# Taking means off weights by an added product, loading weights first, and asking for the last experts' rows sooner, in a fused audio transformer block on Trainium2

## The chip, the cores and the metric

The kernel runs on one core of one Trainium2 chip. The metric is the device time of one execution in microseconds (us). Runs are marked fast or slow by their granted TensorE clock and time; every run in this document is of the fast state. Within that state the time still moves by up to 6.6 us from run to run (a_fetch below), and why it does so is one of the things that this study is about.

## The reference, cut to what matters

64 clips of 80,000 samples are cut into 157 frames of 512 samples. Each frame is turned by an orthonormal DCT; then one layer with an attention-like read and one layer of experts follow, each behind a normalisation and with a residual.

```python
frames = x.reshape(64, 157, 512)              # after padding
h = einsum('bfh,kh->bfk', frames, DCT)        # 512 x 512
y = layernorm(h)
V = y @ Wv + bv; gate = sigmoid(y @ Wg + bg)  # 512 x 512 each
key, query = phases of tanh(y @ Wk), tanh(y @ Wq)   # 32 columns each
# ... causal read of V by key and query phases and by positions, mixed by gate
h = h + (read / norm) @ Wo + bo
z = layernorm(h)
scores = softmax(mean(z, frames) @ Wg2 + bg2); e = argmax(scores)   # one of 16 experts per clip
h = h + scores[e] * (z @ We[e] + be[e])       # 512 x 512 for each clip
```

## The kernel before

The 64 clips go in 16 groups of four. A group has five tiles of tokens (four of 128 and a ragged one, `TAIL`). All products are 32-bit, on TensorE; DVE (VectorE), ACT (ScalarE) and POOL (GpSimd) do the elementwise work. The frames' DCT is done with folds on DVE (`fold_once`, `fold_twice`: sums and differences of parts of a frame) and products with small tables (`embed`). In the code cuts, `bank` and `psum` give pieces of the memory that TensorE writes its products to, `value` is a tile's product with Wv, and `spread` and `scale` multiply a tile of frames by each token's factor of the normalisation (`rstd`). To apply Wv, Wk, Wq and Wg to the *frames* rather than to the DCT's output, the first group turns these weights by the same DCT once, and takes off their mean over the 512 inputs, so that the layer norm's mean need not be taken off the tokens. This happens in `through_dct`:

```python
    load_half(0, 0)                              # frames of group 0, first half
    dct_e = load("dct_e", [P, 2, P]); trig_o = ...; lift = ...
    raw_v = load_raw("wv", D)
    tables = ...                                 # the DCT tables
    load_half(0, 1)
    raw_kq = load_raw("wkq", 2 * F); ...; raw_g = load_raw("wg", D)

    def through_dct(raw, to, n, summed=False):
        if summed:
            ...                                  # two additions on GpSimd, for Wg
        ps = bank()[:, :n]
        ...
            for c in range(C):                   # C = 4 chunks of 128 inputs
                nc.tensor.matmul(ps, mean, raw[:, c], start=(c == 0), stop=(c == C - 1))
        sub(raw, raw, ps.unsqueeze(1).to_broadcast([P, C, n]))      # DVE, 2048 columns for Wv
        yield
        ...                                      # six DCT products, copied out by ACT
```

`first_values` interleaves this with the first group's embeddings, statistics and values; `first_gate` makes the first group's four gate parts beside the embeddings of group 1:

```python
    def first_gate():
        made = chain(weight_sums(wo, t_o), weight_sums(wv, t_v), weight_sums(wg, t_g))
        for n in range(NM):
            embed(1, n)
            embed_statistics(1, n)
            if n == 0:
                fold_twice(1, 1)
            if n < C:
                gate_part(0, n)
            embed_res(1, n)
            ...
```

At the end of a group, an expert is picked for each clip, and its weights (1 MB each) are fetched by indirect DMA, issued by GpSimd with row numbers that DVE works out. For the last group nothing is left to hide this behind, so its four weights come in eight halves:

```python
    def picks(c):
        if c == 1:
            route_spread(g)
            pick(g)
    ...
    expert(g - 1, ORDER[2], picks)               # third expert tile of the group before
    spare = ...
    fetch(g, [...], parts=2)                     # rows on DVE, eight gathers on GpSimd
    pick_gate(g)
    bias(g)                                      # ninth gather, the experts' biases
    for n in (3, 4):
        add_bias(g - 1, ORDER[n])
        expert(g - 1, ORDER[n])
    last = psum()
    banks = [*(bank() for _ in range(3)), last[:, 0, :], last[:, 1, :]]
    for c in range(C):                           # chunk outside, tile inside
        for n in range(NM):
            if c == 0:
                add_bias(g, n)
            expert_chunk(g, n, c, banks[n])
            if c == C - 1 and n != 3:
                for m in (n,) if n < 3 else (3, 4):
                    expert_out(g, m, banks[m])
```

Of the kernel before, what the change touches and what calls it, by code (L numbers as in the profile page):

```python
# [14 lines left out]
F32 = mybir.dt.float32  # L15
# [36 lines left out]
def audio_tower(ctx: ExitStack, tc: tile.TileContext, a, out):  # L52
# [79 lines left out]

    load_half(0, 0)
# [3 lines left out]

    def load_raw(name, n):
        t = p1.tile([P, C, n], F32, tag="we", name=name, bufs=GB)
        nc.sync.dma_start(out=t, in_=a[name])  # L140
        return t

    raw_v = load_raw("wv", D)
    tables = p1.tile([P, 6, P], F32, tag="we", name="tables", bufs=GB)
    nc.sync.dma_start(out=tables, in_=a["tables"])
    load_half(0, 1)
    raw_kq = load_raw("wkq", 2 * F)
# [38 lines left out]
    def through_dct(raw, to, n, summed=False):  # L186




        if summed:
            total = p1.tile([P, 2, n], F32, tag="x2T", name="total")
            nc.gpsimd.tensor_tensor(total, raw[:, :2], raw[:, 2:], ALU.add)
            nc.gpsimd.tensor_tensor(total[:, 0], total[:, 0], total[:, 1], ALU.add)
            yield
        ps = bank()[:, :n]
        if summed:
            nc.tensor.matmul(ps, mean, total[:, 0], start=True, stop=True)
        else:
            for c in range(C):  # L200
                nc.tensor.matmul(ps, mean, raw[:, c], start=(c == 0), stop=(c == C - 1))
        sub(raw, raw, ps.unsqueeze(1).to_broadcast([P, C, n]))
        yield
        for k, parts in enumerate((((0, 1), (1, 3)), ((2, 1), (3, 3)), ((4, 0),), ((5, 2),))):
            if k % 2 == 0:
                ps = psum()
            for i, (table, r) in enumerate(parts):
                nc.tensor.matmul(
                    ps[:, k % 2, :n], tables[:, table], raw[:, r], start=(i == 0), stop=(i == len(parts) - 1)
                )  # L210
            if k % 2:
                nc.scalar.copy(to[:, k - 1 : k + 1], ps[:, :, :n])  # L212
                yield
# [396 lines left out]
    def output_product(g, i):  # L610
# [11 lines left out]
        elif i == 6:  # L622
            add(first, ps, first)
        elif i == 7:
            add(second, ps, first)
            more(r22, second)
            more(r21, second)
            more(r12, first)
        elif i == 5:
            add(r22, ps, r22)  # L630
            for n in (2, 3):
                statistics2(g, n)
            add(r12, ps, r12)
        elif i == 3:
            add(r12, ps, r12)
        else:
            add(r21, ps, r21)
# [76 lines left out]
    def fetch(g, rooms=(), parts=1):  # L714
# [6 lines left out]
        for k in range(parts):  # L721
            rows = t("rows", [P, GB], I32)
            base = rowbase[:, parts + k - 1 : parts + k]
            nc.vector.tensor_scalar(rows, s["rev"], float(-P * parts), base, ALU.mult, ALU.add)
            for b in range(GB):
# [78 lines left out]
    def first_values():  # L804

        consts = constants()
        turn_v = through_dct(raw_v, wv, D)
        turn_kq = through_dct(raw_kq, wkq, 2 * F)
        turn_g = through_dct(raw_g, wg, D, summed=True)

        def embedded(n):
            embed_statistics(0, n)
            embed_res(0, n)

        warm(20)
        fold_once(0, 0, nc.vector)
        fold_twice(0, 0)
        embed(0, 0)
        embed(0, 1)
        embedded(0)  # L820
        next(turn_v)
        embedded(1)
        next(turn_v)
        next(turn_v)
        fold_once(0, 1, nc.vector)
        value(0, 0)
        fold_twice(0, 1)
        keep_value(0, 0)
        embed(0, 2)
        embedded(2)  # L830
        value(0, 1)
        spread(0, 0)
        scale(0, 0)
        embed(0, 3)
        keep_value(0, 1)
        embedded(3)
        embed(0, TAIL)
        embedded(TAIL)
        next(turn_g)
        next(turn_kq)  # L840
        value(0, 2)
        spread(0, 1)
        scale(0, 1)
        next(turn_kq)
        next(turn_kq)
        keep_value(0, 2)
        value(0, 3)
        spread(0, 2)
        scale(0, 2)
        next(consts)  # L850
        keep_value(0, 3)
        value(0, TAIL)
        spread(0, 3)
        scale(0, 3)
        keep_value(0, TAIL)
        spread(0, TAIL)
        scale(0, TAIL)
        fold_once(1, 0)
        next(turn_g)
        project(0)  # L860
        fold_phases(0)
        next(turn_g)
        next(turn_g)
        next(consts)
        fold_twice(1, 0)
        fold_once(1, 1)
        phasors(0)
        next(consts)
        next(consts)
        weigh()  # L870

    def first_gate():

        made = chain(weight_sums(wo, t_o), weight_sums(wv, t_v), weight_sums(wg, t_g))
        for n in range(NM):
            embed(1, n)
            embed_statistics(1, n)
            if n == 0:
                fold_twice(1, 1)
            if n < C:  # L880
                gate_part(0, n)
            embed_res(1, n)
            add_bo(0, n)
            if n < C:
                for _ in range(3):
                    next(made)
            if n > 0:
                spread(1, n - 1)
                scale(1, n - 1)
            if n == 1:  # L890
                scores(0)
        load_half(2, 0)
        load_half(2, 1)

    def project_and_values(g):
# [5 lines left out]
        made = token_sums(g)  # L901
        next(made)
# [18 lines left out]
        keep_product(g)  # L921
        route(g - 1)
        route_sum(g - 1)
        value_product(g, 5)
        keep_product(g)
        route_spread(g - 1)
# [60 lines left out]
    def attention(g):  # L987
# [11 lines left out]
        for i in (1, 2, 6, 7, 4, 5, 3):  # L999
            output_product(g, i)  # L1000
            if i == 1:
# [4 lines left out]
                if g == 0:  # L1006
# [174 lines left out]
```

## Time and profile before

| | |
|---|---|
| time, median of 3 | 1436.16 us (1435.90 to 1436.41) |
| span of the profiled run | 1433.1 us, mean granted clock 0.997 |
| opening: start to the first output product of group 0 | 99.53 us |
| middle: from there to the same product of the last group | 1263.98 us |
| tail: from there to the end | 69.64 us |

I cut the span at two landmarks, the first product of Wo with gated values in the first group and in the last. They stand in the trace of every kernel here (line 361 before, line 362 in the changed kernel), so the three parts can be compared between kernels: opening, middle, tail. The tail holds the last group's output, its routing, the experts of the two last groups and the last stores.

A line of a timeline reads: start, length, engine, line of the kernel, operation, result and operands, shape, number of instructions, and in brackets how long the engine had stood idle ahead of it and what ended that. A line of the table of stretches has the stretch, its length, the busy time and instructions of PE, PEld, DVE, ACT and POOL, the granted clock, the DMA share and GB/s.

### The profile page before, as it was taken

The page shows a single profiled execution, that of the slowest core. Times are in us where ns is not written, and L with a number is a line of the kernel's source. Part 1 is how long each engine was busy: PE and PEld are TensorE (multiplying, and loading weights), DVE is VectorE, ACT ScalarE, POOL GpSimd, SP SyncE. Part 2 cuts the span into 40 slices and gives each one's busy share as a digit, 9 for nine tenths or more (in the row PEclk, how much of TensorE's full clock was granted, in tenths as well). Part 3 has the DMA queues.
Part 4 walks back from the last instruction along what each step waited for, and adds up shares of the span by engine and source line. Part 5 has one row for each costly group of instructions (what it writes and reads, how often), then busy time and mean ns, then how long its engine had stood idle before and what let it go on. Part 6 is the DMA issues. An engine that isn't in the chain of part 4 may idle for free.

```text
span 1433.1 us, 26995 instructions
## 1 busy us (share of the span) xinstructions
PE 1409.2 (98%) x10662; PEld 929.6 (65%) x10662; DVE 995.8 (69%) x2088; ACT 401.0 (28%) x691; POOL 607.3 (42%) x849
## 2 busy tenths in 40 slices
PE   8989999999999999999999999999999999999997
PEld 5567586675757657586675757657585675757751
DVE  4677676777767677676777767677677777767562
ACT  1414233142421314232142422314232142422310
POOL 2355443545445255433535445255433535445222
PEclk9999999999999999999999999999999999999999
DMA  6012304132040322304132040322304132030305
GB/s 210 1 38 78 113 9 148 52 125 74 5 179 16 126 74 86 108 7 157 42 125 74 13 171 16 126 74 95 102 3 163 36 126 74 22 126 16 125 17 182
DMA packets 46941, 119.47 MB, mean 83 GB/s; under 512 B 9232, under 2 KB 26144, under 8 KB 38752
## 3 DMA queue, kind: packets, MB, share of 16 engines
q0 software_dynamic: 11072, 71.31, 13.1%
q1 hardware_dynamic: 35244, 45.80, 10.8%
q8 instruction: 85, 1.39, 0.4%
q10 hardware_dynamic: 500, 0.64, 0.2%
q14 instruction: 40, 0.33, 0.1%
HBM read 97.14 MB, written 20.58 MB: 82 GB/s over the span
## 4 chain that ended last, share of the span: by engine, by line
PE 90%; DVE 4%; POOL 3%; issue 1%; ACT 1%; DMA 1%; DVEq 0%; POOLq 0%
PE mm L361 27%; PE mm L772 16%; PE mm L566 16%; PE mm L600 9%; PE mm L232 8%; PE mm L670 3%; PE mm L513 2%; PE mm L247 2%; PE mm L249 2%; POOL rstd L224 1%; PE mm L680 1%; PE mm L585 1%; DVE st L219 1%; PE mm L287 1%; POOL rstd L223 1%
## 5 line engine op out<-in xcount | busy, mean ns | idle before, releaser
L223 POOL TENSOR_SCALAR rstd<-mv 128x1 f32<-128x1 f32 x160 | 54.4, 340 | 547.9 <-DVE mv L221 535.1
L772 PE MATMUL mm<-we,x2T 128*32 128x512 f32 x2400 | 273.2, 595 | 0.8 <-DVE res_t L783 0.8
L772 PEld LDWEIGHTS mm<-we,x2T 128*32 128x32 f32 x2400 | 70.4, 109 | 149.5 <-issue 142.9
L97 DVE TENSOR_TENSOR gT<-mm,gT 128x128 f32<-128x128 f32 (+1 forms) x135 | 87.0, 673 | 89.8 <-PE mm L566 88.4
L608 DVE TENSOR_TENSOR gT<-mm,gT 128x320 f32<-128x320 f32 x256 | 116.8, 487 | 20.9 <-PE mm L600 16.5
L600 PE MATMUL mm<-att,v 32*128 32x192 f32 (+2 forms) x2048 | 128.0, 371 | 1.3 <-ACT res_t L276 1.0
L600 PEld LDWEIGHTS mm<-att,v 32*128 32x128 f32 x2048 | 105.8, 185 | 12.1 <-PE mm L600 3.0
L726 POOL DMA_INDIRECT we<-in_we,rows x60 | 64.3, 1072 | 103.9 <-issue 98.1
L97 DVE TENSOR_TENSOR v<-mm,v 128x512 f32<-128x512 f32 x105 | 71.0, 688 | 53.4 <-PE mm L361 53.4
L576 ACT ACTIVATE gT<-gT,hbg 128x320 f32<-128x320 f32 x120 | 59.6, 554 | 169.4 <-DVE gT L97 169.4
L224 POOL TENSOR_TENSOR rstd<-rstd,power 128x1 f32<-128x1 f32 x160 | 99.0, 619 | 13.3
L97 DVE TENSOR_TENSOR res<-mm,res 128x512 f32<-128x512 f32 x96 | 64.3, 684 | 56.7 <-POOL res L615 41.8
L276 ACT ACTIVATE res<-mm,shift,rstd 128x512 f32<-128x512 f32 x64 | 49.7, 777 | 165.6 <-POOL rstd L262 124.1
L783 DVE SCALAR_TENSOR_TENSOR res<-mm,gate,res 128x512 f32<-128x512 f32 x64 | 48.1, 751 | 61.6 <-PE mm L287 36.6
L657 ACT ACTIVATE x<-res,shift,rstd 128x512 f32<-128x512 f32 x64 | 52.1, 815 | 137.9 <-DVE res L97 121.3
L361 PE MATMUL mm<-t_o,sum 128*128 128x256 f32 x384 | 88.4, 379 | 0.0
L361 PE MATMUL mm<-t_v,sum 128*128 128x256 f32 x360 | 86.7, 384 | 0.0
L281 POOL TENSOR_TENSOR res<-res,bo 128x512 f32<-128x512 f32 x64 | 86.5, 1380 | 0.2 <-issue 0.2
L361 PEld LDWEIGHTS mm<-t_o,sum 128*128 128x128 f32 x384 | 71.9, 190 | 11.3 <-DVE sum L96 0.4
L615 POOL TENSOR_TENSOR res<-res,u 128x512 f32<-128x512 f32 x48 | 59.6, 1269 | 44.9 <-DVE u L97 44.9
L232 PE MATMUL mm<-wv,xT 128*128 128x512 f32 x160 | 72.2, 594 | 1.3 <-ACT wv L212 0.8
L361 PEld LDWEIGHTS mm<-t_v,sum 128*128 128x128 f32 x360 | 64.8, 190 | 10.7 <-issue 3.7
(195 smaller groups left out, 2770.2 us busy)
## 6 DMA issues: line engine op xcount, KB each, us to landing
xT<-in_frames SPq DMA_DIRECT2D x32, 640.0 KB
out<-res SPq DMA_DIRECT2D x248, 64.0 KB
out<-res_t SPq DMA_DIRECT2D x62, 32.0 KB
out<-res_t SPq DMA_DIRECT2D x62, 26.0 KB
wv<-in_wv SPq DMA_DIRECT2D x1, 1024.0 KB
wg<-in_wg SPq DMA_DIRECT2D x1, 1024.0 KB
wo<-in_wo SPq DMA_DIRECT2D x1, 1024.0 KB
we<-in_we,rows POOLq DMA_INDIRECT x60
```

The costliest lines, as they stand in the source:

```text
L97: add = lambda *x: nc.vector.tensor_tensor(*x, ALU.add)
L223: nc.gpsimd.tensor_scalar(rstd, mv[:, 1:2], EPS, None, ALU.add)
L224: nc.gpsimd.tensor_tensor(rstd, rstd, power, ALU.pow)
L232: nc.tensor.matmul(ps, tile_of(x[:, c], n), w[:, c, :], start=(c == 0), stop=(c == C - 1))
L281: nc.gpsimd.tensor_tensor(r, r, bo, ALU.add)
L361: nc.tensor.matmul(ps[:, b, :], lhs[:, c, P * b : P * (b + 1)], w[:, c, :], start=(c == 0), stop=(c == 1))
L566: nc.tensor.matmul(ps[:, o, :HN], w[:, c, o * P : (o + 1) * P], rhs[:, c], start=(c == 0), stop=(c == 1))
L576: nc.scalar.activation(to, to, AF.Tanh, bias=hbg[:, c : c + 1], scale=0.5)
L600: nc.tensor.matmul(to, s["v", n][q, c * P : (c + 1) * P], by, start=(n == 0), stop=(n == TAIL))
L608: nc.vector.tensor_tensor(th, r[:, :, n], th, op)
L726: nc.gpsimd.indirect_dma_start(out=ws[b][:, n * k : n * (k + 1)], out_offset=None, in_=of, in_offset=bass.IndirectOffsetOnAxis(ap=rows[:, ...
L772: nc.tensor.matmul(ps[Q * i : Q * (i + 1), :], s["x2T"][:, c, i, Q * n : Q * (n + 1)], s["ws"][i][:, c, :], start=(c == 0), stop=(c == C - 1),
```

## The change

The intent is to have TensorE start on real work sooner and wait less in the opening, and to have the last group's expert weights arrive sooner. It has six parts:

1. Tables and Wv are loaded ahead of the frames; Wv in two halves, the odd chunks first.
2. Wv and Wkq go through the DCT as loaded. Their mean comes off at the end: DVE adds up the four chunks, and one more product per output part, with the tables' sums over minus 512, accumulates in the same bank. Wg keeps its subtraction.
3. The order of the first group's work and of its gate parts changes; the gate part comes ahead of the embedding in `first_gate`.
4. DVE's four sums of Wg for the fast products (`t_g`) move from the first gate into group 1.
5. The last group's gathers are requested inside `picks`, with the bias gather between the halves.
6. The last block takes two chunks for all tiles, then the other two tile by tile, the ragged tile first. In the last group one addition (`r12`) stands ahead of two statistics.

```diff
+    tables = p1.tile([P, 6 + C, P], F32, tag="we", name="tables", bufs=GB)
+    nc.sync.dma_start(out=tables[:, :6], in_=a["tables"])
+    raw_v = load_raw("wv", D, (slice(1, C, 2), slice(0, C, 2)))
     load_half(0, 0)
 ...
+    nc.sync.dma_start(out=tables[:, 6:], in_=a["table_sums"].partition_broadcast(P))
+    raw_kq = load_raw("wkq", 2 * F)
     load_half(0, 1)
 ...
+    def less_mean(total, k, to):
+        nc.tensor.matmul(to, tables[:, 6 + k], total, start=False, stop=True)
+
+    def centre(raw, total):
+        ps = bank()
+        nc.tensor.matmul(ps, mean, total, start=True, stop=True)
+        sub(raw, raw, ps.unsqueeze(1).to_broadcast([P, C, D]))
 ...  (first_values)
+        for k in range(2):
+            through_dct(raw_v, k, of[k], stop=False)
+        total = add_up(raw_v, D, "x2T")
+        for k in range(2, C):
+            through_dct(raw_v, k, of[k], stop=False)
+        total_kq = add_up(raw_kq, 2 * F, "sum2")
         fold_once(0, 0, nc.vector)
         fold_twice(0, 0)
+        for k in range(C):
+            less_mean(total, k, of[k])
 ...  (first_gate)
+        made = chain(weight_sums(wo, t_o), weight_sums(wv, t_v))
+        for n in range(C):
+            gate_part(0, n)
             if n == 0:
                 fold_twice(1, 1)
+            m = n + 2
+            if m < NM:
+                embed(1, m)
 ...  (the last group)
     def picks(c):
         if c == 1:
             route_spread(g)
             pick(g)
+            fetch(g, [*flat, all_v.rearrange("p i c o -> p (i c o)")], 2, biases)
 ...
-    fetch(g, [*flat, all_v.rearrange("p i c o -> p (i c o)")], parts=2)
-    pick_gate(g)
-    bias(g)
 ...
+    order = [TAIL, *range(TAIL)]
+    for c in range(2):
+        for n, ps in zip(order, banks):
+            expert_chunk(g, n, c, ps)
+    for n in order:
+        add_bias(g, n)
+    for n, ps in zip(order, banks):
+        for c in range(2, C):
+            expert_chunk(g, n, c, ps)
+        expert_out(g, n, ps)
```

## The prediction

> **What bounds the kernel now.** I read the page first. TensorE is busy nearly all the span and the chain that ended last lies on it.
>
> ```profile
> PE 1409.2 (98%) x10662; PEld 929.6 (65%) x10662; DVE 995.8 (69%) x2088; ACT 401.0 (28%) x691; POOL 607.3 (42%) x849
> ...
> PE 90%; DVE 4%; POOL 3%; issue 1%; ACT 1%; DMA 1%; DVEq 0%; POOLq 0%
> ```
>
> So an average tells nothing here: only TensorE's work, or the little time it waits, can change the time. The busy table by stretches of time says where it waits (columns: stretch in us; its length; busy us of the five engines; granted clock; DMA share; GB/s).
>
> ```profile
> 7.70:99.50 91.80, 80.27 (x503) 50.48 (x503) 59.41 (x125) 27.27 (x46) 38.11 (x60) 0.98 0.23 80
> 99.50:1402.20 1302.70, 1300.58 (x9961) 867.86 (x9959) 926.36 (x1949) 372.49 (x644) 563.55 (x776) 1.00 0.24 81
> 1402.20:1408.60 6.40, 3.74 (x14) 0.45 (x11) 0.00 (x0) 0.00 (x0) 4.69 (x5) 0.90 0.99 345
> ...
> 76.10:79.50 3.40, 3.40 (x7) 2.20 (x8) 3.28 (x7) 0.06 (x1) 1.19 (x3) 0.50 0.02 5
> ```
>
> The reader is to see that 1300.6 of the middle 1302.7 us are busy: fifteen of sixteen groups offer nothing. The waits lie in the first group (up to 99.5 us) and after 1402 us, and twice the clock falls to 0.50. The timeline of TensorE names the waits (start, length, instructions, idle before).
>
> ```profile
> 16.58 5.42 PE L208 MATMUL mm<-wv,tables 128*128 128x512 f32 x12 [2.38 <-DVE wv L96]
> 49.66 2.37 PE L513 MATMUL mm<-xT,wkq 128*64 128x320 f32 x16 [0.73 <-DVE xT L293]
> 76.06 6.26 PE L547 MATMUL mm<-xT,wg 128*128 128x320 f32 x16 [3.87 <-ACT res L276]
> 93.48 1.40 PE L600 MATMUL mm<-att,v 32*128 32x320 f32 x22 [0.99 <-ACT res_t L276]
> 99.53 1.99 PE L361 MATMUL mm<-wo,gT 128*128 128x256 f32 x8
> ...
> 1402.53 1.02 PE L772 MATMUL mm<-wv,x2T_last 128*32 128x512 f32 x2 [0.28 <-DMA wv<-in_we,rows]
> 1405.43 1.05 PE L772 MATMUL mm<-wg,x2T_last 128*32 128x512 f32 x2 [1.88 <-issue]
> 1406.97 1.60 PE L772 MATMUL mm<-spare,x2T_last 128*32 128x512 f32 x2 [0.50 <-issue]
> ```
>
> The first line is the pass that takes the means off Wv: DVE subtracts for 2.3 us while TensorE stands. The line at 99.53 marks the end of the first group's opening, 99.53 us. The last three are the last group's expert weights arriving one by one. The timeline of DVE and GpSimd shows why they come late:
>
> ```profile
> 1395.45 0.75 DVE L783 SCALAR_TENSOR_TENSOR res<-mm,gate,res 128x512 f32<-128x512 f32 x1 [1.43 <-PE mm L772]
> 1396.12 0.35 DVE L724 TENSOR_SCALAR rows<-rev,rowbase 128x4 int32<-128x4 f32 x2
> ...
> 1397.13 1.07 POOL L726 DMA_INDIRECT wv<-in_we,rows  x1 [11.45 <-DVE expf L743]
> 1398.51 1.05 POOL L726 DMA_INDIRECT wg<-in_we,rows  x1 [0.30 <-issue]
> ```
>
> The expert was picked at 1394.02, but the row numbers stand in DVE's queue behind an addition that waits for TensorE.
>
> **What the Trainium skill says.** "TensorE: Matmul & The Clock Gate", Part 1: the clock is judged in free-running windows of 3413 ns, an idle window halves it for the next. The trace agrees: both 0.50 stretches last 3.41 us, follow an idle stretch (3.87 us; 6.3 us with three short bursts), and stretch 16 passes at line 547 from 4.47 to 6.26 us. "GPSIMD Engine Reference", 3.1: a 2048-element fp32 addition takes DVE 2293 ns, GpSimd 4497. The trace has 2.29 us for the DVE subtraction of 2048, 2.34 us on GpSimd for 1024: agreed. "DMA: Bandwidth & Descriptors", Anatomy of one DMA: about 2.0 us plus bytes / 436e3. That gives 3.2 us for a half gather of 512 KB; here the first took 5.4 us (1397.13 to 1402.53) and the fourth 7.5. The measurement decides.
>
> **The change part by part.** I list the queues of the built program, with what each instruction waits for, and lay durations of this trace on them.
>
> *Mean of Wv and Wkq.* Before: 4+4 matmuls with the mean matrix ahead, then a DVE subtraction. After: 4+4 correction matmuls behind, accumulated in the same bank. A 128x512 matmul is two passes of 0.43 us, so 4 x 0.86 = 3.44 us go and 3.44 come: no work is saved, but the 2.4 us wait and 2.29 us of DVE go. What DVE adds is 1.3 + 0.7 us of sums, beside the six DCT matmuls (5.2 us).
>
> *Load order.* Tables (384 KB) and Wv's halves (512 KB each) now precede the frames. The before trace moves about 350 to 400 KB per us from 2.3 us on and reports landings some 0.6 to 1.3 us after the bytes. So tables and first half land near 5.3, the second half near 6.8, the frames near 8.6, the table sums near 10.6, Wkq near 11.0. Warm-up falls from 40 to 24 passes and ends near 5.5 (14 cold at 0.21, 10 at 0.11). TensorE then starts real work at about **5.6** instead of 7.72, and its ten Wv matmuls run to 14.2, under which the fold of the frames (3.7 us of DVE from 11.5, held by Wkq's sum) nearly hides.
>
> *TensorE work from there to line 361's first product*, the same in both: Wv 8.6, Wkq 2.3, five values 17.2, ten embeddings 8.9, spreads 1.1, Wg 6.0, projection 2.3, position scores and scores 2.0, four gate parts 17.2, read 7.5; sum 73.2. Before: 99.53 - 7.72 - 73.2 = 18.6 us of waits and slow clock.
>
> *Waits I expect after.* First tile's second trig matmul 0.3. Values 2 and 3 wait for the scaling of tile 0, for res of tile 2 and res of tile 3: 0.9 + 0.5 + 0.8. The Wg subtraction (kept, 2.29 us on DVE) now stands before the last spread and ahead of the value it must keep: 3.0. That gap fills a clock window, so 1.7 us of slow clock at 8 in 10: 1.4. Tile 2 of group 1 needs fold_twice of the second half, which stands on DVE behind both statistics and behind weigh, that is behind eight Sin activations (4.2 us after a 1.28 us table load): TensorE ends gate part 0 near 60, the fold comes near 62.5 to 64: 3.4, and slow clock at even odds: 0.8. Start of the read, behind the last scalings: 1.5. Wake-ups: 0.9. Sum 13.5. Line 361 then starts at 5.6 + 73.2 + 13.5 = 92.3: **7.2 us gained**. The wait of 3.87 us moves and shrinks rather than vanishes.
>
> *t_g sums* (4 x 0.68 = 2.7 us of DVE) move from the first gate into group 1's value products. There DVE has gaps of 0.5 and 1.6 us and TensorE does not wait on what is delayed by 1.4 us; I charge 0.2.
>
> *Last gather.* Rows come after the pick: 1394.06 instead of 1396.12, so all gathers start 2.06 us earlier. The bias gather goes between the halves (+1.24 us for the second), but the second half is used 8.6 us after the first. TensorE starts the last block at 1406.5 by the old clock, not 1408.57: 2.1. The slow clock there cost 1.1 (two pass pairs at 0.855 and one at 0.65 instead of 0.43); with a shorter gap at even odds: 0.5.
>
> *Last block in another order.* Work is the same 20 x 0.86 us. Before, two tiles' outputs (4 + 8 transfers) hung on the last matmul: its DVE addition is at 1427.02, a second one follows, then six issues on each queue until 1430.7. After, one tile with two issues per queue: 1427.02 + 0.75 + 0.9 + 2.1 to land + 0.8 to close, about 1431.5 against 1433.1: 1.6. Tail: **4.2 us gained**. The earlier r12 addition I count as nought: its gain is a bank's release, its cost 0.7 us on two statistics.
>
> Sum: 7.2 + 4.2 - 0.2 = 11.2; with half a us given for later small shifts, 1436.2 - 11.7 = 1424.5.
>
> **Rivals.** (1) DVE becomes the bound of the opening: it is busy 59.4 of 91.8 us, and the new order stacks Wkq's sum, two statistics and the constants ahead of what TensorE needs. For it: the two new waits of 3 us. If they double, 1430 to 1432. (2) All waits of the opening go, as the change intends: then line 361 starts near 82 and the time is about 1414. Against: the Wg subtraction is still there. (3) The tail is bound by the gather's transfers, not its start: the DMA share is 0.99 from 1402 to 1408. If bytes alone set it, an earlier start still moves them, since the engines carried only 83 to 240 GB/s before 1400; so I keep most. If not, 1427.
>
> **Range and chances.** The opening may gain 3 to 12 us, the tail 2 to 5.5; together 5.5 to 17.5, so 1418.5 to 1430.5 holds it 8 times in 10. Faster by 2% needs 28.7 us; all waits outside the middle are 18.6 in the opening, 7.4 before the last block and 6 at the end, so nearly all would have to go: 0.01. Slower by 2% would need damage in the steady groups, whose order is unchanged: 0.005.
>
> **What would show it.** Right: the first matmul on Wv's raw tiles near 5.6; line 362 (old 361) near 92; a TensorE wait of about 3 us on the Wg subtraction near 42 to 45 and of 3 us on the fold near 60 to 64, with 0.50 clock behind the first; the first of the last gathers 2 us earlier against the last group's picks; the last addition to the end shorter by 1.6. The middle groups stay at their 86 to 87 us each. Wrong: if table sums or the second half of Wv land late and TensorE waits before 14 us; if the waits near 44 or 62 are absent; if the middle groups change.

## The result, and the profile after

| | before | after |
|---|---|---|
| median of 4 runs | 1436.29 us (1435.90 to 1440.82) | 1424.24 us (1423.01 to 1425.31) |
| ratio of the fast runs | | 0.9909, 95% interval 0.9887 to 0.9930 |
| span of the profiled run, clock | 1433.1 us, 0.997 | 1421.9 us, 0.998 |
| opening / middle / tail | 99.53 / 1263.98 / 69.64 us | 93.64 / 1263.65 / 64.65 us |

A ratio is the mean time of one kernel's fast runs over the mean time of the other's in the same rounds, so it is not quite the ratio of the medians. The measured 1424.24 us is 0.3 us from the predicted 1424.5; the range and the class (within 2%) held.

First the page of the changed kernel: its busy times, and the engines' shares of the chain that ended last.

```profile
PE 1405.3 (99%) x10646; PEld 929.2 (65%) x10646; DVE 997.3 (70%) x2090; ACT 402.0 (28%) x690; POOL 607.1 (43%) x849
...
PE 91%; DVE 3%; POOL 3%; DMA 1%; issue 1%; ACT 0%; SPq 0%; DVEq 0%; POOLq 0%
```

TensorE's busy time fell by only 3.9 us (1409.2 to 1405.3), part of it warm-up (sixteen passes fewer) and part time at half clock. The rest of the 11.2 us is idle time gone. The busy table by stretches says where:

```profile
7.00:93.64 86.64, 79.25 (x505) 50.54 (x505) 61.06 (x127) 27.89 (x45) 37.70 (x60) 0.98 0.27 90
93.64:1357.29 1263.65, 1262.31 (x9683) 847.70 (x9681) 902.72 (x1895) 366.82 (x635) 550.15 (x754) 1.00 0.24 82
...
1395.60:1400.30 4.70, 3.08 (x13) 0.36 (x8) 0.75 (x1) 0.00 (x0) 3.11 (x4) 1.00 0.95 334
...
65.30:68.70 3.40, 3.40 (x8) 2.42 (x9) 0.83 (x3) 2.44 (x4) 0.00 (x0) 0.50 0.00 0
```

The middle is as full as before. Idle time in the opening fell from 11.5 (91.8 less 80.3) to 7.4 us. The stretch between the arrivals of the first and the fourth expert weight is 4.7 us long at full clock; before it was some 6 us with the clock at 0.90. There is one stretch of half clock in the opening, as before, but in another place. The timeline of TensorE names what waits are left in the opening:

```profile
7.00 5.50 PE L196 MATMUL mm<-wv,tables 128*128 128x512 f32 x12 [0.15 <-DMA wv<-in_wv]
...
45.62 0.30 PE L288 MATMUL mm<-ident,rstd 128*128 128x128 f32 x1 [2.36 <-DVE wg L96]
46.19 5.42 PE L196 MATMUL mm<-wg,tables 128*128 128x512 f32 x12 [0.28 <-DVE v L411]
63.85 0.84 PE L248 MATMUL mm<-dct_e,xT 128*128 128x128 f32 x4 [2.63 <-issue]
```

The 2.38 us wait for DVE's subtraction from Wv, ahead of line 208 before, is gone, and Wv's DCT now begins at 7.00 instead of 16.58 us. The two waits that the prediction named are there: for the subtraction from Wg (2.36 and 0.28), and near 61 us for the fold of group 1's second half (2.63; the profile shows no releaser for it, and the built program has the instruction wait for that fold on DVE and for a bank that ACT frees). In the tail, the row numbers and gathers of the last group:

```profile
1387.55 0.41 DVE L728 TENSOR_SCALAR rows<-rev,rowbase 128x4 int32<-128x4 f32 x2
...
1388.57 1.07 POOL L732 DMA_INDIRECT wv<-in_we,rows  x1 [8.73 <-DVE logit L744]
...
1393.68 0.95 POOL L762 DMA_INDIRECT be<-in_be,expi  x1 [0.30 <-issue]
```

The rows now follow right behind the pick (its last step ends at 1387.51); before they stood 2.1 us behind it in DVE's queue. Measured from the last group's first output product, the first gather is issued at 31.28 us instead of 33.62. TensorE still waits for the halves, but shortly:

```profile
1396.85 1.04 PE L778 MATMUL mm<-wg,x2T_last 128*32 128x512 f32 x2 [0.27 <-DMA wg<-in_we,rows]
1398.80 1.05 PE L778 MATMUL mm<-spare,x2T_last 128*32 128x512 f32 x2 [0.90 <-DMA spare<-in_we,rows]
1400.28 0.62 PE L778 MATMUL mm<-t_v,x2T_last 128*32 128x512 f32 x1 [0.44 <-DMA t_v<-in_we,rows]
```

So in these two profiles 5.9 us came out of the opening, 0.3 out of the middle and 5.0 out of the tail. A pair of profiles is one draw of the clock's windows, though, and the experiments show that this draw is worth several us.

### The profile page after: what moved, and what is told of

The parts are those of the page before. It is cut to its first block, busy times and chain, and to the rows that moved or that the text cites. A ratio compares the mean times of both kernels' runs of the same rounds, so it can differ in the third digit from the quotient of the medians.

```text
span 1421.9 us, 26962 instructions
## 1 busy us (share of the span) xinstructions
PE 1405.3 (99%) x10646; PEld 929.2 (65%) x10646; DVE 997.3 (70%) x2090; ACT 402.0 (28%) x690; POOL 607.1 (43%) x849
## 4 chain that ended last, share of the span: by engine, by line
PE 91%; DVE 3%; POOL 3%; DMA 1%; issue 1%; ACT 0%; SPq 0%; DVEq 0%; POOLq 0%
PE mm L362 26%; PE mm L567 16%; PE mm L778 16%; PE mm L601 9%; PE mm L233 8%; PE mm L674 3%; PE mm L514 2%; PE mm L248 2%; PE mm L250 2%; PE mm L684 1%; POOL rstd L225 1%; PE mm L586 1%; PE mm L548 1%; PE mm L288 1%; DVE st L220 1%
## 5 line engine op out<-in xcount | busy, mean ns | idle before, releaser
L119 POOL TENSOR_TENSOR xT<-xT 128x640 f32<-128x640 f32 x30 | 46.5, 1550 | 59.7 <-DVE even L97 40.7
```

## The experiments

Twelve kernels ran, in three calls on three chips, each with five rounds and a profile. The kernel before ran beside them; its mean was 1437.1, 1438.2 and 1437.5 us. This table has all of them, with the time as median, and the parts of the one profiled run. "Slow" lists the starts of the stretches of half clock in that profile up to the last matmul.

| kernel | median us | ratio to before, 95% | opening | tail | slow from, us |
|---|---|---|---|---|---|
| before (profile) | | | 99.53 | 69.64 | 76.1, 1407.3 |
| after (profile) | 1424.24 | 0.9909 (0.9887 to 0.9930) | 93.64 | 64.65 | 65.3 |
| a_open | 1428.56 | 0.9939 (0.9926 to 0.9952) | 94.92 | 69.21 | 45.9, 66.4, 1401.0 |
| a_tail | 1434.38 | 0.9977 (0.9962 to 0.9992) | 103.08 | 65.97 | 16.9, 40.8, 78.3, 95.4 |
| a_fetch | 1435.91 | 0.9993 (0.9975 to 1.0011) | 103.41 | 70.92 | 17.6, 41.5, 79.0, 96.1, 1413.6 |
| a_block | 1434.82 | 0.9988 (0.9971 to 1.0004) | 99.51 | 69.97 | 76.2, 1407.4 (two windows) |
| again | 1425.21 | 0.9904 (0.9888 to 0.9920) | 95.20 | 64.67 | 46.2, 66.7 |
| b_fold | 1423.99 | 0.9900 (0.9883 to 0.9917) | 93.64 | 64.47 | 47.0 |
| b_wg | 1422.27 | 0.9890 (0.9873 to 0.9908) | 92.59 | 64.32 | 63.7 |
| b_both | 1422.60 | 0.9889 (0.9871 to 0.9906) | 92.05 | 66.34 | 1398.4 |
| u_fetch | 1425.62 | 0.9921 (0.9907 to 0.9935) | 95.00 | 68.94 | 46.3, 66.8, 1401.4 (two windows) |
| u_mean | 1431.90 | 0.9960 (0.9946 to 0.9974) | 102.75 | 65.09 | 9.9, 16.7, 54.3, 74.7 |
| u_load | 1429.13 | 0.9942 (0.9929 to 0.9955) | 98.90 | 65.16 | 9.4, 50.3, 70.8 |
| c_fill | 1423.51 | 0.9906 (0.9890 to 0.9921) | 92.19 | 65.09 | none |

The middle took 1263.94 to 1263.98 us in the kernels with the old opening and 1263.53 to 1263.69 in those with the new one. The 0.38 us lie in the first group alone (86.25 against 85.87 us; every later full group takes 85.83 to 85.84 in both): group 1's ragged tile was spread there before, and is now spread in the opening. So no gain or loss hides in the steady groups, and the theory that the moved `t_g` sums give the opening's gain back falls.

### Which half of the change did it: a_open and a_tail

My theory was that the gains of the opening and of the tail are independent and add up. The rivals were luck of the clock windows, and, for the tail, the transfers' own time. a_open is the changed opening with the old tail, a_tail the old opening with the changed tail.

```diff
 a_open, against the changed kernel
-            fetch(g, [*flat, all_v.rearrange("p i c o -> p (i c o)")], 2, biases)    # and parts 5 and 6 undone
+    fetch(g, [*flat, all_v.rearrange("p i c o -> p (i c o)")], parts=2)
 a_tail, against the kernel before
+            if g + 1 == NG:
+                add(r12, ps, r12)
+            fetch(g, [*flat, all_v.rearrange("p i c o -> p (i c o)")], 2, biases)    # and the block's new order
```

> The opening of the changed kernel (load order, means by an added pass, gate order, sums in group 1) with the tail of the kernel before (late gather, old order of the last block, old place of the r12 addition). Theory, gains add up: the first output product stands at 93.6 us as in the changed kernel, the tail takes from there what it takes before, so the time falls by 5.9 us, to about 1430.3 (ratio 0.996). Rival A, the tail's gain was luck of the clock windows: then this kernel comes out well below 1430, near 1425 to 1428, when its windows fall well. Rival B, the opening's gain is given back by the t_g sums in group 1: then the stretch from the first output product to the last group's is longer than 1264 us and the time is above 1432.

> The opening of the kernel before with the whole tail of the changed one (early gather, biases between the halves, last block in the other order, r12 addition earlier in the last group). Theory: the gain is that of the two profiles' tails, about 5 us, to 1431.0; of it about 1.8 from the gather, 1.1 from a slow clock that does not come, 1.85 at the very end, 0.5 from the r12 addition. Rival, clock luck: the slow clock comes back at the last block in this kernel's profile and the gain is 1.1 us less, near 1432.2. Rival, bytes: the last piece of weights lands as late as before, and only the end's 1.85 us remain, near 1434.

Measured: a_open has the ratio 0.9939, some 8.8 us of 1437; a_tail 0.9977, some 3.3 us. Together that is 12.1 us, and the whole change took off 13.1 (0.9909) and, in its repetition, 13.8 (0.9904). Within their intervals of about 2 us the halves add up, and the opening is the larger half. The amounts are not those that I expected from the two profiles (5.9 and 5): the opening gives more, the tail less. For a_tail the median, 1434.38 us, is the number of the rival with the transfers (near 1434) and not that of the theory (1431.0).

The profile of a_tail shows one cause of the larger opening. Its opening is that of the kernel before, instruction for instruction, and yet it took 103.08 us, not 99.53. The busy table by stretches:

```profile
16.90:20.30 3.40, 3.40 (x5) 1.34 (x5) 3.30 (x7) 0.00 (x0) 2.41 (x4) 0.50 0.39 90
40.80:44.20 3.40, 3.40 (x5) 1.35 (x4) 0.00 (x0) 0.00 (x0) 3.26 (x4) 0.50 0.00 0
78.30:81.70 3.40, 3.40 (x8) 2.22 (x7) 3.30 (x8) 0.00 (x0) 1.19 (x3) 0.50 0.02 5
95.40:98.80 3.40, 3.40 (x38) 3.23 (x42) 0.00 (x0) 0.00 (x0) 3.40 (x4) 0.50 0.02 5
```

Four stretches at half clock (0.50), where the profile of before has one. All starts lie whole multiples of 3.413 us apart, so the windows stand on a fixed grid (the free-running window of 3413 ns that the Trainium skill has in "TensorE: Matmul & The Clock Gate", Part 1; the trace agrees), and this grid begins anywhere with respect to the kernel: 1.04 us into a window's length in the profile of before, 3.21 in a_tail, 0.53 in a_fetch. In these profiles it matters where a wait falls in the grid. The wait of 2.4 us for Wg lies whole within the window from 42.8 to 46.3 us in the profile of again, and the next window is slow; in that of after a window ends at 44.8 us, inside the same wait, and neither neighbour is slow. Laid beside each other from Wv's products on, the same instructions of before and a_tail drift apart only inside slow windows; waits in between take some of it back, and 3.5 us are left behind the last window. The old opening took 99.53, 99.51, 103.08 and 103.41 us in its four profiles, mean 101.4; the new one 93.64, 95.20, 94.92 and 95.00 (after, again, a_open, u_fetch), mean 94.7. The gain of the opening is 6.7 us between these means. The profile from which the prediction started had a lucky grid. (By time, a_open's gain is 8.8 us, 6.9 to 10.6 by its interval; the 6.7 us here and the 0.4 us of the middle make 7.1.)

### The two parts of the tail: a_fetch and a_block

```diff
 a_fetch, against the kernel before: the early gathers and the biases between their halves, nothing else
 a_block, against the kernel before: the last block's new order, nothing else
```

> The kernel before with one part of the change: the last gathers requested right after the pick, the bias gather between their halves. Theory: the gathers start 2 us earlier and the last block's end moves with them: 1.8 us faster, 2.9 where the slow clock at the last block does not come, so 1433.4 to 1434.5. Rival, the transfers set the end: the fourth half still lands near the old time and the gain is below 0.5 us.

> The kernel before with one part of the change: the last block in the other order (each tile's third and fourth products together, the ragged tile first, the biases added between). Theory: TensorE's work on the last block starts and ends as before; from its last addition on DVE to the end it is 4.2 instead of 6.1 us, so 1.85 us faster, near 1434.4. Rival: the new order makes TensorE wait for a second half that it needs earlier, or DVE's five additions of biases stand ahead of the outputs, and the gain is below 1 us.

By time neither can be told from the kernel before: 0.9993 (0.9975 to 1.0011) and 0.9988 (0.9971 to 1.0004). The times are inconclusive at this size; the profiles tell more. In a_block, the last matmul is followed by 4.23 us up to the end, instead of 6.17; in a_open and a_fetch, which have the old order, 6.31 and 6.21, in the changed kernel 4.30. So behind the last matmul the new order is worth 1.9 us, as expected. In a_block's own profile this was lost again: its tail is 69.97 us against 69.64, because the last matmul ended 65.7 instead of 63.5 us after the last group's first output product, with the fourth weight in use 1.0 us later and two slow windows in place of one. In a_fetch, the first gather is issued at 31.58 us after the last group's first output product instead of 33.62, also as expected, but the weights then came late. The timeline of TensorE:

```profile
1409.68 1.04 PE L774 MATMUL mm<-spare,x2T_last 128*32 128x512 f32 x2 [1.83 <-DMA spare<-in_we,rows]
1413.02 0.62 PE L774 MATMUL mm<-t_v,x2T_last 128*32 128x512 f32 x1 [2.30 <-DMA t_v<-in_we,rows]
```

The fourth weight's first half was issued at 1402.80 and used at 1413.02, 10.2 us later; in before that took 7.5 us (1401.11 to 1408.57). This ate the earlier start. In that stretch the stores of the group before ran beside the gathers: twelve of 64 KB were issued 1.7 to 9.5 us after the first gather, against five, up to 4.2 us after it, in the kernel before. So I formed the rival theory that the earlier gathers lose their gain by sharing the DMA engines. I tested it with u_fetch. The kept traces settle one part of it: after, again, b_fold, b_wg and b_both have the same twelve stores, at the same 1.7 to 9.5 us after the first gather, and there the fourth weight was in use 7.5 to 8.0 us after its issue. So these stores alone do not make it late.

### The early gathers, undone in the changed kernel: u_fetch

```diff
 against the changed kernel
-            fetch(g, [*flat, all_v.rearrange("p i c o -> p (i c o)")], 2, biases)
 ...
     expert(g - 1, ORDER[2], picks)
+    fetch(g, [*flat, all_v.rearrange("p i c o -> p (i c o)")], 2)
+    biases()
```

> The changed kernel with one part undone: the last gathers stand again where the kernel before has them, behind the third expert of the group before, and the bias gather behind all of them. Theory (the start of the gather sets when the last block can go on): 1.8 to 2.1 us slower than the changed kernel, about 1426.5, and the fourth weight comes into use 44.6 us or more after the last group's first output product instead of 42.8 to 43.2. Rival, found in a_fetch (there the earlier gathers shared the engines with the stores of the group before, each half took 9 to 10 instead of 7.5 us to land, and only about 1 us of time came off): nearly all is lost to sharing, and undoing it costs less than 1 us, about 1425.

The mean of the runs is 1426.75 against 1424.76 us of the changed kernel in the call before (on another chip): 2.0 us lost, the number of the theory. It is not clear of the noise: the ratios, 0.9921 and 0.9904, have intervals that overlap. The runs fall in two: 1425.05, 1425.55 and 1425.62 us at clocks of 0.997 to 0.999, and 1428.23 and 1429.30 at 0.996 and 0.994. The timeline of TensorE in the profiled run, one of the latter:

```profile
1399.97 1.04 PE L778 MATMUL mm<-wg,x2T_last 128*32 128x512 f32 x2 [1.73 <-DMA wg<-in_we,rows]
1402.29 1.92 PE L778 MATMUL mm<-spare,x2T_last 128*32 128x512 f32 x2 [1.28 <-issue]
```

Two products take 1.92 us instead of 1.04: half clock, behind the wait. So in this profile the late gather costs twice, by its wait and by the slow windows that follow it. The three runs near 1425.3 us did not pay the second price in full: a slow window of 3.41 us takes 0.0012 off the mean clock of 1425 us, so a clock of 0.999 leaves room for about one in all. Over all profiles: with late gathers the fourth weight comes into use 44.93 to 46.04 us after the last group's first output product (before, a_open, a_block, u_fetch), and all four have at least one slow window in the last block. With early ones it comes into use 42.35 to 45.66 us after it (ten profiles, mean 43.2), and two of ten have a slow window there. The two latest (44.38 in a_tail, 45.66 in a_fetch) are on one chip, both with the old opening. So the sharing rival is not needed for the other eight, where the fourth half was in use 7.2 to 8.0 us after its issue, much as with late gathers (7.3 to 8.2); what made it 9.2 and 10.2 us in those two is **open**. The gain in use is 2.1 us between the means (45.3 to 43.2); all early ones but a_fetch have the earlier `r12` addition too, which no run has by itself (with it, u_fetch's late gather starts at 33.35 instead of 33.62 us).

### The added product against the subtraction: u_mean

```diff
 against the changed kernel
-        for k in range(2):
-            through_dct(raw_v, k, of[k], stop=False)
-        total = add_up(raw_v, D, "x2T")
-        ...
+        subtract_mean(raw_v, D)     # four products with the mean matrix, then DVE subtracts, as before
+        for k in range(C):
+            through_dct(raw_v, k, of[k])
 ...   # the same for Wkq, its mean products ahead of the embeddings
```

> The changed kernel, its load order and order of work kept, but the means of Wv and Wkq taken off as in the kernel before: four products with the mean matrix ahead, then DVE's subtraction from the raw weights, no added pass. Theory of the prediction (no TensorE work is saved, the gain is DVE's 2.3 us subtraction that TensorE waits for): a wait of 2.4 us comes back ahead of Wv's first DCT product, the first output product 2.1 to 2.4 us later, 3.8 where a slow clock follows the wait; 1426.5 to 1428. Rival: the fold of the frames (landed at 10.6 us, 3.7 us of DVE) sets the pace there anyway and less than 1 us is lost.

Measured: a mean of 1431.93 us, 7.2 us more than the changed kernel in the call before (the ratios, 0.9960 and 0.9904, have intervals that lie apart), twice to three times what I had expected. The timeline of TensorE shows why:

```profile
8.74 5.37 PE L214 MATMUL mm<-wv,mean 128*128 128x512 f32 x8 [2.00 <-DMA wv<-in_wv]
16.49 7.11 PE L196 MATMUL mm<-wv,tables 128*128 128x512 f32 x12 [2.38 <-DVE wv L96]
```

The subtraction's wait is there as expected, 2.38 us. But the mean needs all four chunks, and its first product takes chunk 0, which is in the half of Wv that lands second, so it starts at 8.74 instead of 7.0 us. And both waits were followed by half clock: the mean's products take 5.37 us (3.67 in before), the DCT's 7.11 (5.42 in before). The sum, 1.7 + 2.4 + 1.7 + 1.7 = 7.5 us, is the difference of the openings (102.75 against 95.20). So the added product does more than cover DVE's subtraction: it lets the DCT begin on half of the weights, at full clock.

### The order of the loads: u_load

```diff
 against the changed kernel
+    load_half(0, 0)
+    dct_e = ...; trig_o = ...; lift = ...
     tables = ...
     raw_v = load_raw("wv", D, (slice(1, C, 2), slice(0, C, 2)))
-    load_half(0, 0)
-    dct_e = ...; trig_o = ...; lift = ...
```

> The changed kernel with the first loads in another order: frames and embedding tables ahead, then the DCT tables and Wv's two halves, as in the kernel before. Theory (with Wv first in the order of work, its landing is what TensorE's start hangs on): Wv's first half lands near 9.3 instead of 6.0 to 6.9 us, the start moves from 6.5 or 7.0 to about 9.5, and 2.5 to 3 us are lost, more if the clock falls back while TensorE waits: 1427 to 1429. Rival: the folds and frames, then earlier, take up what the late start loses, and the time is within 1 us of the changed kernel.

Measured: a mean of 1429.18 us, 4.4 more than the changed kernel (ratios 0.9942 and 0.9904, intervals apart). The timeline of TensorE:

```profile
9.22 7.08 PE L196 MATMUL mm<-wv,tables 128*128 128x512 f32 x12 [2.73 <-DMA wv<-in_wv]
```

The start moves from 7.0 to 9.22 us, and the wait brings half clock again (7.08 instead of 5.50 us): 2.2 + 1.6 = 3.8 us, and the openings differ by 3.7 (98.90 against 95.20, with the same two later slow windows). The folds do not take it up. Neither u_mean's 7.2 nor u_load's 4.4 us can be added to the other: each undoes one of two parts that only work together. No run undoes part 3, the order of the first group's work and of its gate, by itself, so its own share of the opening's gain is not shown.

### The waits that are left: b_wg, b_fold and b_both

The control of this call is the changed kernel itself:

> The changed kernel once more, as the control of this call and as a second profile. Theory of additive gains (opening 8.8 by a_open's times, tail 3.3 by a_tail's): about 12 us below the kernel before, ratio 0.9915, the middle again 1263.6 to 1264 us. In the profile the first output product stands between 92 and 97 us depending on how the clock's windows fall over the waits near 44 and 63 us; if the windows' phase does not matter, it stands at 93.6 again.

Its opening was 95.20 us, not 93.64, on another grid. The timeline of TensorE has the same wait on Wg as before and, behind it, what the first profile had not:

```profile
45.58 0.29 PE L288 MATMUL mm<-ident,rstd 128*128 128x128 f32 x1 [2.36 <-DVE wg L96]
46.15 7.11 PE L196 MATMUL mm<-wg,tables 128*128 128x512 f32 x12 [0.28 <-DVE v L411]
```

7.11 instead of 5.42 us at half clock: these 1.69 us are all by which this opening is longer (1.56). a_open (7.04) and u_fetch (7.11) show it as well, so it came in three of four profiles.

```diff
 b_wg, against the changed kernel
         keep(2)
+        centre(raw_g, total)
+        value(0, TAIL)
         next(consts)
-        value(0, TAIL)
         fold_once(1, 0)
-        centre(raw_g, total)
 b_fold, against the changed kernel
         phasors(0)
+        fold_twice(1, 1)
         for n in range(2):
             embed_res(1, n)
         weigh()
 ...
-            if n == 0:
-                fold_twice(1, 1)
```

b_both has both moves.

> The changed kernel with the mean of Wg taken off two steps earlier (its matmul and DVE's subtraction are emitted ahead of the constants and the ragged tile's value product, which then runs on TensorE meanwhile). Theory of the prediction (the subtraction stands bare before the value it must keep): the waits of 2.36 and 0.28 us near 45 us go, and with them the slow clock that follows them in some runs: 2 to 3 us faster than the changed kernel. Rival: the bank for the mean's matmul comes free late and the sum on GpSimd is not ready, so TensorE waits ahead of it instead: 0 to 1 us.

> The changed kernel with one line moved: the second half's fold_twice of group 1 is emitted right behind the phasors and ahead of weigh, so that DVE does not do it behind the eight Sin activations. Theory of the prediction (the wait of TensorE near 62 us hangs on this fold on DVE): the wait of 2.63 us shrinks by about 1.6 us and the window near 62 us is busy enough that no slow clock follows: 1.5 to 3 us faster than the changed kernel, first output product at about 91.5. Rival: the gate part behind it waits for res of tile 1 on ACT, which itself stands behind the Sin activations; then the wait changes its releaser and at most 0.6 us come off.

> Both moves together. Theory: they add up, the first output product near 89 to 90 us, 4 to 5 us faster than the changed kernel, about 1420. Rival: waits are handed on to the start of the read (behind the last scalings on ACT and GpSimd), which only moves: then both together bring no more than the better of the two.

Measured, as means: again 1424.76, b_wg 1422.59, b_fold 1423.92, b_both 1422.75 us. Moving the subtraction is worth 2.2 us (95% interval of the difference 0.8 to 3.5). Moving the fold gives 0.8 alone, which is within the noise (-0.4 to 2.1), and nothing on top: my theory that the two moves add up, to about 1420, failed, and its rival held. The timeline of TensorE in b_wg:

```profile
40.12 3.70 PE L233 MATMUL mm<-wv,xT 128*128 128x512 f32 x8 [0.48 <-ACT res_t L277]
45.64 5.42 PE L196 MATMUL mm<-wg,tables 128*128 128x512 f32 x12 [1.60 <-DVE v L411]
```

The rival had a part in it: of 2.64 us of waits 2.08 are left, now for a bank that ACT frees and for DVE's queue behind the subtraction. What went is the long wait in one piece, and with it the slow window: none of the three profiles with this move (b_wg, b_both, c_fill) has half clock near 45 us. (All three happen to stand at much the same place of the grid, 2.1 to 2.3 us into a window; at other places this is not shown.) In b_fold (timeline of TensorE):

```profile
63.48 0.84 PE L248 MATMUL mm<-dct_e,xT 128*128 128x128 f32 x4 [0.96 <-PE mm L548]
66.39 4.57 PE L548 MATMUL mm<-xT,wg 128*128 128x320 f32 x16 [0.91 <-ACT res L277]
```

Here the rival was right as well. The 2.63 us become 0.96, and 0.91 us come back two instructions later as a wait on ACT, which has the eight Sin activations ahead of it. (The slow window of this profile at 47.0 lay behind Wg and none followed at 65 us.)

### What the slow window is worth: c_fill

```diff
 c_fill, against b_wg, in the first group's first gate part
+        if g == 0 and o == 0:
+            for _ in range(9):
+                nc.tensor.matmul(ps[:, 1, HN : HN + P], ident, ident, start=True, stop=True)
```

> The kernel b_wg (mean of Wg taken off earlier) with nine idle products of the identity behind the first group's first gate part, in unused columns of its bank: they do no work that is used, they only keep TensorE busy in 1.9 of the 2.6 us in which it waits for the fold near 61 us. Theory (the wait itself costs 2.6 us and the half clock that follows it another 1.6): no window near 60 to 68 us is slow, the first output product stands at about 91.0 instead of 92.6 us, the time is about 1420.7. Rival: the slow window after the wait costs little beside what ACT and DVE would have kept TensorE waiting for anyway; then the time is that of b_wg, 1422.3.

The idle products are in columns that nothing reads; they only keep the clock up. They did: the profile has no slow window before the last store phase, and the mean granted clock of the four timed runs was 0.999 to 1.000. But the time did not fall: a mean of 1423.59 us, ratio 0.9906 against 0.9890 of b_wg (the intervals overlap, the chips differ), and the opening is shorter by 0.40 us, not 1.6. The timelines of TensorE, first b_wg:

```profile
65.51 5.28 PE L548 MATMUL mm<-xT,wg 128*128 128x320 f32 x16
...
72.79 4.47 PE L548 MATMUL mm<-xT,wg 128*128 128x320 f32 x16
```

and c_fill:

```profile
65.04 4.47 PE L548 MATMUL mm<-xT,wg 128*128 128x320 f32 x16
...
71.59 0.32 PE L288 MATMUL mm<-ident,rstd 128*128 128x128 f32 x1 [0.17 <-ACT res L277]
72.28 4.58 PE L548 MATMUL mm<-xT,wg 128*128 128x320 f32 x16 [0.36 <-ACT gT L559]
```

The second gate part ends 1.3 us sooner (69.5 against 70.8), but then two waits on ACT come up, 0.53 us together, and where the third gate part starts 0.51 us of the lead are left. So the same slow window that cost 1.7 us behind Wg's wait costs 0.4 us here, where ACT is close behind TensorE.

## Why the prediction was right, point by point

**The start.** The step said 5.6 us for TensorE's first real product. It was 6.05 to 7.00 us in the eight profiles with the new opening (7.00 in after). Two terms were off. The 24 warm-up passes took 4.6 to 5.5 us, ending at 6.0 to 6.9; the prediction ended them near 5.5 with 14 cold passes, but in the changed kernel's profile the clock rose only at 7.2 us (at 4.4 in that of before) and all 24 ran cold. And Wv's first half landed at 5.6 to 6.9 us, not at 5.3. The prediction read 350 to 400 KB per us out of the trace of before; over 2.3 to 9.0 us that trace has 302 GB/s, with some 240 to 250 from 5 to 7 us. In the changed kernel's profile, 14 of the 16 completions of this load had come by 5.4 us, the last two at 6.6 and 6.9. Cost: 0.4 to 1.4 us. One of the prediction's signs of being wrong showed in small: before 14 us TensorE waited for the table sums for 0.2, 0.4 and 0.8 us in b_wg, u_fetch and b_both.

**The opening as a whole.** 92.3 us were predicted; 93.64, 95.20, 94.92 and 95.00 measured. The gain was predicted as 7.2 us from the one profile of before; between the means of four profiles each it is 6.7. The size held, though by errors on both sides: the new opening was 1.3 to 2.9 us later than predicted, and the old one is on the average 1.9 us later than the profile that the prediction had. The two large terms of the sum were off, in opposite senses. TensorE's work was put at 73.2 us (its terms add up to 73.1); of the 79.25 us busy some 77.5 are left without the slow window's 1.7. The read took 9.0 us busy instead of 7.5, the ten embeddings 10.3 instead of 8.9 (b_both, with no slow window there). Waits and slow clock were put at 13.5 us and measured 9.1 (7.4 idle, 1.7 slow). For before, the same sum gave 18.6 us of waits and slow clock, where the prediction's own stretch has 91.80 - 80.27 = 11.5 us idle and a slow window 1.7. So that 92.3 came near is in part luck; the gain, a difference of two such sums, was harmed less. Between the two profiles the start gave 0.7 us instead of 2.1, waits and slow clock 4.1 instead of 5.1, and TensorE's work 1.0 instead of nothing.

**The waits in it.** Wg's subtraction: predicted 3.0, measured 2.64. The slow clock behind it: predicted 1.7 at 8 in 10, measured 1.6 to 1.7 in three of four profiles. The fold near 61 us: predicted 3.4, measured 2.63. The slow clock there: predicted at even odds, measured in four of four, but worth 0.4 us rather than 1.7 (c_fill). Values 2 and 3: predicted 2.2, measured 0.78 and 0.27. The start of the read: predicted 1.5, measured 0.52 and 0.35. The single waits were mostly over-estimated; the wait after the fold was also put down to one cause where two stood one behind the other (b_fold).

**The clock.** The prediction saw an idle stretch ahead of both slow windows of before. Ahead of the first, at 76.1 us, the window was 0.02 busy; ahead of the second, at 1407.3, it was 0.41 busy (see the last section).

**The mean's mechanism.** "No work is saved, but the 2.4 us wait and 2.29 us of DVE go" was right and incomplete. u_mean shows the wait at 2.38 us, and beside it 1.7 us of landing and 3.4 us of half clock that the added product avoids.

**The t_g sums.** Charged 0.2; no loss is to be seen in group 1, which is as long as the others (85.84 us; the prediction said 86 to 87 for the middle groups of both kernels).

**The last gather.** 2.06 us earlier was predicted; the gathers start 2.0 to 2.3 us earlier, and the fourth weight comes into use 2.1 us earlier between the means. The slow clock at the last block: predicted 0.5 us (even odds of 1.1); it came in all four profiles with the late gather and in two of ten with the early one. Rival 3, the transfers, held in two profiles on one chip only, and its cause there is open.

**The end.** 1.6 us predicted, 1.9 measured (6.2 to 4.3 us from the last matmul on). The tail as a whole: 4.2 predicted, 69.4 to 65.1 us measured between means (late gather with the old order: before and a_open; both parts changed: nine profiles), so 4.3. By time a_tail gave 3.3 us (1.1 to 5.5 by its interval), on the chip where its gathers were slow.

**The sum.** Between the two profiles the opening gave 5.9 us instead of 7.2, the tail 5.0 instead of 4.2, and the middle 0.3, where half a us had been allowed for small shifts. That the time came within 0.3 us of the prediction is in part that these errors cancel.

**The rivals.** DVE as bound of the opening (1) did not come: its two waits stayed at 2.6 us each. All waits gone (2) did not come either; b_both and c_fill, which remove most of what can be removed by order, are at 1422.6 and 1423.5.

**A better version.** b_wg is the fastest: a median of 1422.27 us, ratio 0.9890 to before, and its mean 2.2 us below that of the changed kernel in the same call.

## What to carry to other kernels

Where a constant correction (here a mean) can be applied by one more accumulated product *behind* the main ones, TensorE need not wait (2.4 us here) for an elementwise pass ahead of them, and can start on whatever part of the weights has landed; load order and order of work must then be changed together. When TensorE is the bound, look for single waits of about 2.4 us and longer: in these runs each cost its length and, depending on where it fell in the clock's grid, up to 1.7 us more, so that moving one paid 2.2 us although the sum of waits shrank by 0.6 only (b_wg). Compare means over several profiles before reading a part's gain from one pair of traces, because the same instructions took 99.5 or 103.4 us here.

## What the Trainium skill lacked or had wrong

- "TensorE: Matmul & The Clock Gate", Part 1, has the clock fall after an idle window; its second failure mode has frequent short idle times do it too, but it gives no share. The runs show shares: over the profiles, with the busy intervals of TensorE added up in each 3413 ns slot of the grid, every whole slot up to 0.42 busy was followed by half clock, of the 23 between 0.43 and 0.63 ten were and thirteen were not, and of those above only two were, both slow themselves (0.69 and 0.75).
- The same part calls the ramp a cost under 1% of a typical kernel's span and says not to fit a model to a count of cold matmuls. That holds here (3.9 us are 0.3% of the span), but a change can be as small: the grid's place moves equal instructions from 99.5 to 103.4 us in the opening, as much as parts of the change. The page's free-running window, and its varying number of cold passes (24 warm-up passes took 4.6 to 5.5 us), agree with the runs.
- No page says what a slow window is worth when another engine is close to being the bound: 1.7 us behind Wg's wait, 0.4 us in the gate parts.
- "DMA: Bandwidth & Descriptors", Anatomy of one DMA, has a fit for one DMA from GpSimd by itself; worked out for 512 KB it is the estimate of 3.2 us that the prediction quotes. With four such gathers in a row the fourth was in use 7.2 to 8.2 us after its issue in twelve profiles, and 9.2 and 10.2 us after it in two. A figure for gathers that queue behind each other is missing, and so is one for queued loads from SyncE: Wv's first half, behind 384 KB of tables, landed 4.4 to 5.7 us after its issue (issued at 1.2, landed at 5.6 to 6.9).
